# A graph network's first layer: its update from sums split along the node and across it, with products and factors moved into the pair loop

## The chip, the cores and the metric

The kernel runs on one core of a Trainium2 chip. The metric is the device time of one execution in microseconds. Each kernel is run several times and the median is taken.

The engines are PE (TensorE: `matmul` and transposes), DVE (VectorE: elementwise work and reductions), ACT (ScalarE: functions such as sigmoid, logarithm, square root), POOL (GpSimd: elementwise work, and the issue of some transfers) and SP (SyncE, which here only issues transfers). Each has its own queue and works it off in order. SBUF is the memory on the core, 128 partitions wide; PSUM is the memory that PE writes to. A DMA moves data between these and the chip's main memory.

## The reference

Four graph layers run on 4096 nodes with 128 features and one symmetric adjacency matrix of 4096 x 4096. Each is followed by a residual sum and a layer norm. The change concerns the first:

```python
mv = proj(mobius_matvec(weight, x))
h = proj(mobius_add(mv, hyp_bias))                 # 4096 x 128, points of a ball
x_tangent = logmap0(h)
x_local = jax.vmap(lambda xi: logmap(xi, h))(h)    # 4096 x 4096 x 128, never stored
logits = (x_tangent @ wl)[:, None] + (x_tangent @ wr)[None, :] + att_b[0]
adj_att = adj * jax.nn.sigmoid(logits)
support_t = jnp.einsum('ij,ijd->id', adj_att, x_local)
h_agg = proj(expmap(h, support_t))                 # the update
out = proj(expmap0(h_agg))
...
x = _layernorm(x + out)
```

`mobius_add(x, y)` is a sum of x and y with two factors for each row, made from x·x, x·y and y·y. `expmap(h, u)` is `mobius_add(h, tanh(lambda |u| / 2) u / |u|)`. So after the sum over the neighbours all that is left for a node is a combination of two vectors, its own point g and its sum v, with factors that follow from a few scalar products. Layer 1 is an attention of four heads masked by the adjacency; layers 2 and 3 are a normalised product and a second attention.

## The kernel before

**Tiles.** The nodes are 32 row tiles of 128 (`NT`) and 8 blocks of 512 (`NS`). `HA` holds g for all nodes with a column of ones, `HT` its transpose, `X` the sums v and later the layer's output.

**The pair loop** (`Fast.pair_loop`, from L1754). The adjacency is symmetric, so it runs over the 36 block pairs I ≤ J. For each it makes distances on PE (`distance`, L1820 and L1823), the elementwise functions on DVE and ACT (`shift` L1829, `mask` L1849, `square` L1852, `ln` L1856, `root` L1860, `inverse` L1864, `add_root` L1868, `log` L1873, `phi` L1877, `sigmoid` L1837, `first` L1881, `second` L1892), transposes (`turn` L1887), and sums on PE: `sum_i` (L1904) collects in PSUM for row block I over the whole row of pairs, `sum_j` (L1919) gives the part for block J of each pair. `add_j` and `add_i` (L1931 for the first row, L1933 later) bring both into X. After `add_i` of row I, block I is complete, since blocks J > I get their last part from row J.

The order of the engines' queues is written by hand: `SHARED_ORDER` (L43) lists the operations of three pairs, each with its place in the step and how many steps it runs ahead, and `manual_schedule` keeps that order. POOL issues the loads of the rows `el` and `er` (L1806, L1812), which `distance` needs, and DMAs that narrow the adjacency to bf16 in main memory (`adjb`, in `narrow`).

**The update** (the end of `layer0`, L519 to L616). For all 32 tiles, in three passes: the sums `gv` = g·v on DVE (L550) and `vv` = v·v on ACT (L553); then w = wg g + wv v with the sum of its squares (`part` L543 and L545, `w` L569, `junk` L576); then w = c2 w + c1 g, again with the sum of squares (L593, L600); at last X = gf w + x0 (L612) and the layer norm of groups of four tiles (`normalise_tile`, statistics L209 and L210, scaling L244). Between the passes stand chains of small operations on columns of 128 x 32, with square roots and hyperbolic tangents on ACT, for which ACT changes its function table. `x0` is the layer's input, loaded by SP when the loop has ended.

**The proof.** The loop is right only for a symmetric adjacency, and `mirror` (L1691, with `compare` L1698) proves this: it fetches blocks I,J and J,I of `adjb` (512 KB each, `low` and `up`, 48 fetches on SP), PE adds one and subtracts the transpose of the other with identity matrices of different sizes (L1735, L1740), and DVE takes the largest absolute value of the result (L1747). Eight pairs were proved before the loop; the other 20 and the 8 diagonal blocks follow after it. `mirror(ctx)` is called ahead of the three passes, so a planner interleaves both by priority.

**Layer 1** (`Fast.layer1`, L2202). X is transposed on PE (L175, evacuated at L190), queries and keys are multiplied (L2255), each result is cut into two parts (`cut`, ACT L2257, DVE L2258), SP stores 16 pieces of 512 KB to main memory (L2264), and POOL loads them again, stacked for the attention (L2233). Values V (L2271) and residual Y (L2281) follow. Layer 1's preparation takes the priority from which the proof started (`self.rank`). Then comes the attention: scores on PE (`ps` L2045), exponential on ACT (L2052), mask on DVE (`e` L2054), products on PE (`pv` L2071).

Of the kernel before, what the change touches and what calls it, by code (L numbers as in the profile page):

```python
# [9 lines left out]
F32 = mybir.dt.float32  # L10
# [51 lines left out]
class Net:  # L62
# [257 lines left out]
    def layer0(self, x, weight, bias, att_w, att_b):  # L320
# [4 lines left out]
        with ExitStack() as ctx:  # L325
# [191 lines left out]
            pre_pools.close()  # L517
            self.pair_loop(HT, HA, dr, rows, adp, early, rows4)

            x0 = HT.rearrange("p (t d) -> p t d", d=D)
            nc.sync.dma_start(out=x0, in_=self.rows(x))
            late = ctx.enter_context(self.pool(name="late0", bufs=1))
            rot = ctx.enter_context(self.pool(name="rot0", bufs=6))
            self.mirror(ctx)
            w = late.tile([P, NT, D], F32, tag="w", name="w")
            gv, vv, wsq = self.col("gv"), self.col("vv"), self.col("wsq")

            def quadratic(name, a, c):  # L530

                q, r = self.tt(name, a, gg, ALU.mult), self.tt(name + "r", c, gv, ALU.mult)
                nc.vector.scalar_tensor_tensor(q, r, 2.0, q, op0=ALU.mult, op1=ALU.add)
                nc.vector.tensor_tensor(q, q, a, ALU.mult)
                nc.vector.tensor_tensor(r, c, c, ALU.mult)
                nc.vector.tensor_tensor(r, r, vv, ALU.mult)
                nc.vector.tensor_tensor(q, q, r, ALU.add)
                nc.vector.tensor_scalar(q, q, MIN_NORM * MIN_NORM, None, op0=ALU.max)
                return q

            def scaled(t, dst, src, factor):
                if t % 8 in (1, 4, 6):
                    nc.gpsimd.tensor_scalar(dst, src, factor, None, op0=ALU.mult)  # L543
                else:
                    nc.scalar.activation(dst, src, AF.Copy, scale=factor)  # L545

            for t in range(NT):
                k = slice(t, t + 1)
                junk = rot.tile([P, P], F32, tag="junk", name="junk")
                nc.vector.scalar_tensor_tensor(  # L550
                    junk, H[:, t, :], 1.0, X[:, t, :], op0=ALU.mult, op1=ALU.mult, accum_out=gv[:, k]
                )
                junk = rot.tile([P, P], F32, tag="junk", name="junk")  # L553
                nc.scalar.activation(junk, X[:, t, :], AF.Square, accum_out=vv[:, k])
            sm = self.tt("sm", gv, b2x, ALU.mult)
            nc.vector.tensor_tensor(sm, sm, self.XA[:, :, D], ALU.subtract)
            nc.vector.tensor_tensor(sm, sm, bhalf, ALU.mult)


            un = self.norm("un", quadratic("uu", sm, bhalf))  # L560
            th = self.act("sg", self.tt("unb", un, rb, ALU.mult), AF.Tanh)
            sg = self.tt("sgu", th, self.rec("run", un), ALU.mult)
            wg, wv = self.tt("wg", sg, sm, ALU.mult), self.tt("wv", sg, bhalf, ALU.mult)
            nc.vector.tensor_tensor(wg, wg, b, ALU.add)
            for t in range(NT):
                k = slice(t, t + 1)
                part = rot.tile([P, P], F32, tag="part", name="part")
                scaled(t, part, X[:, t, :], wv[:, k])
                nc.vector.scalar_tensor_tensor(w[:, t, :], H[:, t, :], wg[:, k], part, op0=ALU.mult, op1=ALU.add)  # L569
                junk = rot.tile([P, P], F32, tag="junk", name="junk")  # L570
                if t % 4 == 3:
                    nc.vector.scalar_tensor_tensor(
                        junk, w[:, t, :], 1.0, w[:, t, :], op0=ALU.mult, op1=ALU.mult, accum_out=wsq[:, k]
                    )
                else:
                    nc.scalar.activation(junk, w[:, t, :], AF.Square, accum_out=wsq[:, k])  # L576
            den = self.ts("den2", th, -1.0, ALU.mult, 1.0, ALU.add)
            nc.vector.tensor_scalar(th, th, 1.0, None, op0=ALU.add)
            nc.vector.tensor_tensor(den, den, th, ALU.mult)
            nc.vector.tensor_tensor(den, den, b, ALU.mult)  # L580
            nc.vector.tensor_tensor(den, den, wsq, ALU.add)
            nc.vector.tensor_scalar(den, den, MIN_NORM, None, op0=ALU.max)
            rden = self.rec("rden2", den)
            c2 = self.tt("c2", rden, b, ALU.mult)
            c1 = self.tt("c1", rden, wsq, ALU.mult)
            nc.vector.tensor_tensor(c1, c1, b, ALU.mult)

            gsq = self.col("gsq")
            for t in range(NT):
                k = slice(t, t + 1)  # L590
                part = rot.tile([P, P], F32, tag="part", name="part")
                scaled(t, part, H[:, t, :], c1[:, k])
                nc.vector.scalar_tensor_tensor(w[:, t, :], w[:, t, :], c2[:, k], part, op0=ALU.mult, op1=ALU.add)  # L593
                junk = rot.tile([P, P], F32, tag="junk", name="junk")
                if t % 4 == 3:
                    nc.vector.scalar_tensor_tensor(
                        junk, w[:, t, :], 1.0, w[:, t, :], op0=ALU.mult, op1=ALU.mult, accum_out=gsq[:, k]
                    )
                else:
                    nc.scalar.activation(junk, w[:, t, :], AF.Square, accum_out=gsq[:, k])  # L600

            gn = self.norm("gn", gsq)
            gf = self.to_ball("gp", gn)
            gn = self.tt("gn2", gn, gf, ALU.mult)
            nc.vector.tensor_scalar(gn, gn, MIN_NORM, None, op0=ALU.max)
            th = self.act("gth", gn, AF.Tanh)
            nc.vector.tensor_tensor(gf, gf, th, ALU.mult)
            nc.vector.tensor_tensor(gf, gf, self.rec("rgn", gn), ALU.mult)
            nc.vector.tensor_scalar(th, th, MIN_NORM, None, op0=ALU.max)
            nc.vector.tensor_tensor(gf, gf, self.to_ball("gp2", th), ALU.mult)  # L610
            for t in range(NT):
                nc.vector.scalar_tensor_tensor(  # L612
                    X[:, t, :], w[:, t, :], gf[:, t : t + 1], x0[:, t, :], op0=ALU.mult, op1=ALU.add
                )
                if t % 4 == 3:
                    self.normalise_tile(t // 4, on_scalar=True)  # L616
# [1038 lines left out]


class Fast(Net):

    MARKS = 160
    waits = "tile"  # L1660
    banks = 5
    EARLY = 8

    def __init__(self, ctx, tc, x, adj, good):
        super().__init__(ctx, tc, x, adj)
# [81 lines left out]
    def mark(self):  # L1749

        self.marks += 1
        return self.odd[:, self.marks - 1 : self.marks]
# [875 lines left out]
```

## Time and profile before

| what | us |
| --- | --- |
| median of 3 runs | 1984.52 |
| the three runs | 1983.38 to 1991.49 |
| the profiled execution's own time | 1991.43 |
| its span, first to last instruction | 1989.6 |
| last addition into X of the pair loop ends | 639.98 |
| first cut of layer 1 starts | 720.60 |
| last cut of layer 1 (ACT) starts | 751.06 |

The mean granted TensorE clock was 0.968. The last three rows are times from the span's start, in the chain of work that ended last. In what follows, a row of a table by windows gives the stretch in us, its length, and for each engine its busy us and number of instructions; at the end stand the TensorE clock, the share of the DMA engines' time and the GB/s moved. A row of waits names the waiting operation, what it waited for, and the us in total, how many times, and the longest. A row of the chain has the start, the us, and the operation. A row of groups has the line, engine, operation, output and input with their shapes and count, then busy us and mean ns, then the idle time before them with what ended it.

The transfers between the loop's end and 770 are 25 `low` and 17 `up` fetches that fall wholly into it, 16 stores of `qk` with a median of 10.5 us from issue to landing, and 20 loads of the stacks of 256 KB, 11.0 us each.

### The profile page before, as it was taken

What the parts mean: (1) busy time and instruction counts of PE and PEld (TensorE: products, weight loads), DVE (VectorE), ACT (ScalarE), POOL (GpSimd) and SP (SyncE); (2) the same over time, 40 slices, a digit from 0 to 9 for tenths busy, and PEclk for the clock granted to TensorE, in tenths of its full rate; (3) what the DMA queues carried; (4) which work ended last, traced back from release to release, by engine and by line L of the source; (5) the groups of instructions that cost most, each with busy time, mean ns of one, the idle gap of its engine ahead of it and who ended that gap; (6) DMA issues with size and microseconds to landing.
All of it is one profiled execution on the core that took longest, in us unless ns stands there. A gap on an engine that the chain in (4) does not pass through costs nothing.

```text
span 1989.6 us, 23419 instructions
## 1 busy us (share of the span) xinstructions
PE 1843.4 (93%) x8408; PEld 991.9 (50%) x8423; DVE 1737.9 (87%) x2726; ACT 1320.4 (66%) x1671; POOL 174.2 (9%) x275
## 2 busy tenths in 40 slices
PE   6779999999998688999999999999999899899997
PEld 5347676667667354333333333333333566544443
DVE  6689989998898866789999999999998988878896
ACT  5699999999997744778787877778777422210000
POOL 2311111121100411200000000000000000000000
PEclk9889999999999989999999999999999999999999
DMA  9778989898945876986867676867667799968882
GB/s 322 169 144 152 170 134 173 148 177 147 154 119 171 338 248 225 293 252 212 239 212 233 211 233 212 232 214 235 213 215 249 312 421 421 421 245 317 291 283 77
DMA packets 172719, 459.25 MB, mean 231 GB/s; under 512 B 13372, under 2 KB 56156, under 8 KB 148016
## 3 DMA queue, kind: packets, MB, share of 16 engines
q1 hardware_dynamic: 117408, 339.13, 47.3%
q0 software_dynamic: 45824, 50.88, 20.0%
q10 hardware_dynamic: 9360, 67.64, 10.6%
q8 instruction: 68, 1.11, 0.2%
q14 instruction: 59, 0.48, 0.1%
HBM read 480.59 MB, written 111.23 MB: 297 GB/s over the span
## 4 chain that ended last, share of the span: by engine, by line
PE 43%; DVE 28%; ACT 17%; DMA 7%; issue 5%; SPq 0%; POOL 0%; ACTq 0%; DVEq 0%; POOLq 0%
PE pv L2071 11%; PE pa L1586 10%; DVE e L2054 9%; PE ps L2045 6%; ACT e L2052 4%; DMA ring<-adjf 3%; PE pj L1919 3%; PE pi L1904 3%; DVE nat L2036 2%; ACT w L1837 2%; PE pz L1820 2%; DVE t L1868 2%; ACT s L1860 2%; ACT nat L2027 1%; PE pa L2441 1%
## 5 line engine op out<-in xcount | busy, mean ns | idle before, releaser
L2054 DVE SCALAR_TENSOR_TENSOR e<-at,e 128x2048 f32<-128x2048 bf16 x256 | 582.6, 2286 | 76.0 <-ACT e L2052 75.5
L2052 ACT ACTIVATE e<-ps 128x1024 f32<-128x1024 f32 x512 | 493.2, 1024 | 149.4 <-PE ps L2045 122.0
L2071 PE MATMUL pv<-e,VA 128*64 128x512 f32 x2048 | 498.2, 607 | 6.0 <-DVE e L2054 5.5
L2045 PE MATMUL ps<-QS,KS 128*128 128x512 f32 x1024 | 314.2, 424 | 8.7 <-ACT e L2052 8.1
L2045 PEld LDWEIGHTS ps<-QS,KS 128*128 128x128 f32 x1024 | 170.4, 188 | 235.6 <-ACT e L2052 177.6
L2071 PEld LDWEIGHTS pv<-e,VA 128*64 128x64 f32 x2048 | 125.1, 136 | 250.5 <-issue 215.7
L1586 PE MATMUL pa<-w,Y 128*128 128x512 f32 x448 | 195.6, 594 | 0.0
L1583 DVE SCALAR_TENSOR_TENSOR w<-rho,col,ring 128x512 f32<-128x512 f32 x224 | 163.0, 746 | 25.1 <-PE pa L1586 12.3
L1820 PE MATMUL pz<-HT 128*128 128x512 f32 x288 | 160.0, 638 | 18.8 <-DVE w L1892 9.8
L1904 PE MATMUL pi<-HA,w 128*128 128x129 f32 x1152 | 154.9, 283 | 9.4 <-DVE w L1881 9.4
L1904 PEld LDWEIGHTS pi<-HA,w 128*128 128x128 f32 x1152 | 141.7, 196 | 20.8 <-issue 16.8
L2423 PE MATMUL pa<-ring,Y 128*128 128x512 f32 x512 | 132.3, 409 | 14.5 <-DVE ring L2398 10.0
L1586 PEld LDWEIGHTS pa<-w,Y 128*128 128x128 f32 x448 | 83.6, 190 | 106.4 <-issue 79.2
L2027 ACT ACTIVATE nat<-nat 128x2048 f32<-128x2048 f32 x64 | 122.6, 1915 | 4.9 <-DMA nat<-in_adj_dram 4.9
L1919 PE MATMUL pj<-HA,w 128*128 128x129 f32 x896 | 118.1, 288 | 2.2 <-DVE X L1933 1.1
L2423 PEld LDWEIGHTS pa<-ring,Y 128*128 128x128 f32 x512 | 95.9, 192 | 44.3 <-DVE ring L2398 12.8
L1919 PEld LDWEIGHTS pj<-HA,w 128*128 128x128 f32 x896 | 110.5, 201 | 10.4 <-issue 7.4
L1829 DVE TENSOR_SCALAR t<-pz 128x512 f32<-128x512 f32 x144 | 93.4, 683 | 14.9 <-PE pz L1823 14.9
L1868 DVE SCALAR_TENSOR_TENSOR t<-t,s 128x2048 f32<-128x2048 f32 x36 | 82.3, 2285 | 20.8 <-ACT s L1860 20.8
L1837 ACT ACTIVATE w<-di,dr 128x512 f32<-128x512 f32 x144 | 90.6, 707 | 0.3 <-DMA di<-rows 0.2
L1892 DVE TENSOR_TENSOR w<-w,ptz 128x512 f32<-128x512 f32 x112 | 73.6, 682 | 18.2 <-PE ptz L1887 17.8
L2387 DVE SCALAR_TENSOR_TENSOR odd<-ring 128x1024 bf16<-128x1024 f32 x64 | 78.1, 1220 | 10.0 <-DMA ring<-adjf 9.5
(419 smaller groups left out, 2351.9 us busy)
## 6 DMA issues: line engine op xcount, KB each, us to landing
ring<-adjf SPq DMA_DIRECT2D x128, 1024.0 KB, 13.8
adjf<-in_adj_dram SPq DMA_DIRECT2D x64, 1024.0 KB, 6.8
nat<-in_adj_dram ACTq DMA_DIRECT2D x64, 1024.0 KB, 5.5
ad<-in_adj_dram SPq DMA_DIRECT2D x36, 1024.0 KB, 8.5
adjb<-in_adj_dram POOLq DMA_DIRECT2D x64, 512.0 KB, 11.6
at<-adjb SPq DMA_DIRECT2D x63, 512.0 KB, 3.5
low<-adjb SPq DMA_DIRECT2D x28, 512.0 KB, 5.2
up<-adjb SPq DMA_DIRECT2D x20, 512.0 KB, 6.3
```

What stands on the lines that cost most here:

```text
L1583: nc.vector.scalar_tensor_tensor(w, rho[:, I * S : (I + 1) * S], col[:, 0, j : j + 1], at[:, jb, :], op0=ALU.max, op1=ALU.mult)
L1586: nc.tensor.matmul(pa, lhsT=F[:, j, :], rhs=w, start=False, stop=(j == NT - 1), skip_group_check=True)
L1820: nc.tensor.matmul(pz, lhsT=HT[:, j * P : (j + 1) * P], rhs=HT[:, I * S : (I + 1) * S], start=True, stop=False)
L1837: nc.scalar.activation(w[:, jb, :], st[p]["d"][k], AF.Sigmoid, bias=dr[:, 4 * J + jb : 4 * J + jb + 1])
L1904: nc.tensor.matmul(row[I, "po"][ib // 2][:, ib % 2, :], lhsT=st[p]["w0"][:, jb, ib * P : (ib + 1) * P], rhs=HA[:, 4 * J + jb, :], start=False,
L1919: nc.tensor.matmul(pj[:, a, :], lhsT=st[p]["w1"][:, ib, jb * P : (jb + 1) * P], rhs=HA[:, 4 * I + ib, :], start=(ib == 0), stop=(ib == 3),)
L2027: nc.scalar.activation(nat, nat, AF.Identity, accum_out=self.deg2[:, k, i : i + 1])
L2045: nc.tensor.matmul(p[:, h, :], lhsT=KS[:, h2 + h, jb * P : (jb + 1) * P], rhs=QS[I % 2][:, h2 + h, :], start=True, stop=True,)
L2052: nc.scalar.activation(e[:, h2 : h2 + 2, :], p, AF.Exp)
L2054: nc.vector.scalar_tensor_tensor(e, at[:, jb % 4, :].unsqueeze(1).to_broadcast([P, NH, S]), 0.0, e, op0=ALU.not_equal, op1=ALU.mult,)
L2071: nc.tensor.matmul(st["po"][h // 2][g : g + 64, :], lhsT=VA[:, o : o + 64], rhs=e[:, h, :], start=(jb == 0), stop=(jb == NT - 1), skip_gro ...
L2423: nc.tensor.matmul(st["pa"], lhsT=halves[k][:, j, :], rhs=at[:, jb, :], start=(I > 0 and j == k == 0), stop=(j == NT - 1 and k == 1), skip ...
```

## The change

The sum v is split into a part along g and a part across it. With gv = g·v and gg = g·g, `along` = -gv/gg, and v + along g is the part across, with ss its square. The update's result is then x0 + ga g + gb (v + along g), with factors ga and gb that follow from gv, ss and gg alone, by column work. No vector w is formed, and no pass takes sums of it.

Blocks of rows 0 to 6 (28 row tiles) are split within the pair loop. As soon as `add_i` has completed block I, the generator `apart(I)` issues a product on POOL; six places of the written order later a reduction and a small product on DVE, and three products on POOL; ten places later a second reduction on DVE. `proceed` is called at each place and also advances `factors` for the first 16 tiles (`SPLIT = 4` blocks) by one small operation, where the square root is made as an exponential of half a logarithm, so that it uses the table that ACT has loaded; hyperbolic tangents are made behind the sigmoids. The first four tiles' outputs are finished in the loop's last part, on DVE.

After the loop follow the sums of the last four tiles, `factors` for the other 16 tiles with square roots, with row tiles between its steps, then the remaining tiles: two fused operations, statistics and scaling. All of this is under `manual_schedule`. Only then is `self.mirror(ctx)` called, where it stood ahead of the passes. `x0` is loaded where the loop's order issues its last loads. The old passes remain as `Net.update`, for the program that runs only where the proof fails.

In the queues that result, SP has 36 of the 48 proof fetches, then the 16 stores, then the other 12 fetches, where all 48 stood ahead of the stores. PE has 306 of the 521 matmuls of the proof ahead of the first query and key product, 36 among these products, 18 among those of the values, 21 about the bound of the scores, and 140 behind the attention's first six scores, where all stood ahead.

```diff
             pre_pools.close()
+            self.given = x, HT, HA, gg, b, rb, b2x, bhalf
             self.pair_loop(HT, HA, dr, rows, adp, early, rows4)
-            x0 = HT.rearrange("p (t d) -> p t d", d=D)
-            nc.sync.dma_start(out=x0, in_=self.rows(x))
-            self.mirror(ctx)
...
+            self.update(ctx)
...
@@ class Fast @@
+    SPLIT = 4
...
+    def factors(self, lo, hi, logs):
...
+        def root(t):
+            nc.vector.tensor_scalar(t, t, MIN_NORM * MIN_NORM, None, op0=ALU.max)
+            yield "root"
+            if logs:
+                nc.scalar.activation(t, t, AF.Ln)
+                nc.scalar.activation(t, t, AF.Exp, scale=0.5)
+            else:
+                nc.scalar.activation(t, t, AF.Sqrt)
...
+        tt(ga, c2, a)
+        tt(gb, c2, q)
...
+    def update(self, ctx):
...
+        def tiles(lo, hi):
+            for t in range(lo, hi):
+                x = X[:, t, :]
+                nc.vector.scalar_tensor_tensor(x, x, gb[:, t : t + 1], x0[:, t, :], op0=ALU.mult, op1=ALU.add)
+                nc.vector.scalar_tensor_tensor(x, HA[:, t, 0:D], ga[:, t : t + 1], x, op0=ALU.mult, op1=ALU.add)
+                self.row_stats(t)
...
+        with self.tc.manual_schedule():
+            tiles(0, 4)
+            last = range(NT - 4, NT)
...
+            for hop in self.factors(4 * self.SPLIT, NT, False):
+                if hop in ("sums", "tanh") and hops < 2 or hop == "root" and hops:
+                    tiles(made, made + 1 + (hops > 0))
+                    made += 1 + (hops > 0)
...
+            for I in range(self.NS):
+                tiles(max(made, 4 * I), 4 * I + 4)
+                if I:
+                    scale(I - 1)
+            scale(self.NS - 1)
+        self.mirror(ctx)
...
@@ Fast.pair_loop @@
+            dotp = ctx.enter_context(self.pool(name="dot0", bufs=1))
+            self.cols_of_update()
+            ahead_of = self.factors(0, 4 * self.SPLIT, True)
+            due, hop = [], None
...
                     for k, po in enumerate(row[I, "po"]):
                         add_up(I, I, k, po)
+                    self.complete = I + 1
+                    if I < NS - 1:
+                        due.append([0, apart(I)])
...
+            def apart(I):
+                c = slice(4 * I, 4 * I + 4)
+                g, v = HA[:, c, 0:D], self.X[:, c, :]
+                prod = dotp.tile([P, 4, D], F32, tag="prod", name="prod")
+                nc.gpsimd.tensor_tensor(prod, g, v, ALU.mult)
+                yield 6
+                nc.vector.tensor_reduce(self.gv[:, c], prod, AX.X, ALU.add)
+                nc.vector.tensor_tensor(self.along[:, c], self.gv[:, c], self.minus[:, c], ALU.mult)
+                prod = dotp.tile([P, 4, D], F32, tag="prod", name="prod")
+                nc.gpsimd.tensor_tensor(prod, g, self.along[:, c].unsqueeze(2).to_broadcast([P, 4, D]), ALU.mult)
+                nc.gpsimd.tensor_tensor(v, v, prod, ALU.add)
+                prod = dotp.tile([P, 4, D], F32, tag="prod", name="prod")
+                nc.gpsimd.tensor_tensor(prod, v, v, ALU.mult)
+                yield 10
+                nc.vector.tensor_reduce(self.ss[:, c], prod, AX.X, ALU.add)
...
+            def proceed(last):
+                nonlocal hop
+                for d in due:
+                    d[0] -= 1
+                if due and due[0][0] <= 0:
+                    wait = next(due[0][1], None)
+                    if wait is not None:
+                        due[0][0] = wait
+                    else:
+                        due.pop(0)
+                        if self.complete >= self.SPLIT:
+                            hop = hop or ""
...
+                hop = next(ahead_of, "end") or ""
...
                 for i in range(-max(reach), n // UNIT - min(reach)):
                     step(i)
+                    if i + max(reach) == n // UNIT - 1:
+                        nc.sync.dma_start(out=x0, in_=self.rows(self.given[0]))
+                while due or hop != "end":
+                    proceed(True)
```

## The prediction

> **What bounds the kernel now.** I read the page's table of engines first (PE 93% busy, DVE 87%, ACT 66% of 1989.6 us), and set it aside: it averages four layers, and the change touches only layer 0 and the step into layer 1. The stages matter, so the second view is the table by windows: the pair loop (79 to 640 us), the three passes of the update, and layer 1's preparation until its attention starts at 767.
>
> ```profile
> core 0: us, PE busy (x) PEld busy (x) DVE busy (x) ACT busy (x) POOL busy (x), PEclk, DMA share, GB/s
> 160.00:600.00 440.00, 424.33 (x2445) 298.30 (x2444) 406.88 (x390) 426.57 (x380) 72.04 (x118) 0.97 0.86 151
> 640.00:648.00 8.00, 6.44 (x72) 4.44 (x69) 8.00 (x64) 7.36 (x51) 0.00 (x0) 1.00 0.79 268
> 648.00:668.30 20.30, 13.97 (x138) 8.76 (x140) 17.11 (x80) 17.37 (x79) 8.35 (x12) 1.00 1.01 381
> 668.30:688.70 20.40, 13.47 (x137) 8.76 (x140) 16.97 (x62) 17.56 (x73) 11.85 (x13) 1.00 1.01 394
> 688.70:720.60 31.90, 21.89 (x190) 16.37 (x194) 24.93 (x130) 15.64 (x44) 0.00 (x0) 0.84 0.45 149
> 720.60:753.00 32.40, 25.07 (x92) 15.00 (x91) 21.82 (x34) 11.47 (x17) 10.90 (x20) 0.84 1.03 332
> 753.00:767.00 14.00, 10.88 (x82) 9.40 (x81) 9.39 (x20) 3.42 (x4) 0.00 (x0) 1.00 0.98 350
> ```
>
> In the loop three engines are nearly full together: ACT 426.57 of 440 (97%), PE 96%, DVE 406.88 (92%). DVE has 33 us to spare, ACT 13. The two middle passes of the update run at a DMA share of 1.01: the symmetry proof's 48 fetches stream beside them. Third view: the waits of ACT and the chain after the loop.
>
> ```profile
> ACT y L1852 <- DVE t L1829: 4.1, 3, 2.9
> ACT t L1873 <- DVE t L1868: 1.1, 4, 0.3
> ```
> ```profile
> 703.85 5.01 DMA low<-adjb
> ...
> 712.08 4.17 DMA low<-adjb
> ...
> 720.60 0.70 ACT cut L2257
> ...
> 728.35 9.41 DMA qk<-cut
> ...
> 739.37 11.58 DMA qk<-cut
> ```
>
> ACT waits for DVE only 5.2 us in 440: DVE is just fast enough. After the loop the chain goes through the columns and passes, then through the proof's fetches (PE's queue holds all of some 520 proof matmuls ahead of the first query/key product), then through the stores of the query/key pieces, which saturate the DMA (332 to 350 GB/s). So the update lies wholly on the path, and what comes behind it is bound by DMA.
>
> **What the Trainium skill says.** "SBUF — State Buffer", section "Who interferes with whom": GpSimd shares its port pair with DVE, a DVE instruction with two SBUF inputs contends with a GpSimd one that reads SBUF, the pair is an exclusive lock, and tensor_reduce never contends. The trace agrees in the one place where both run, before the loop:
>
> ```profile
> 49.87 1.05 DVE L499 TENSOR_TENSOR de<-de,ah 128x32 f32<-128x32 f32 x1
> ```
> ```profile
> 49.84 1.04 POOL L462 TENSOR_TENSOR squares<-HA 128x512 f32<-128x512 f32 x1 [14.33 <-DVE HA L457]
> ```
>
> A 128x32 product (0.18 to 0.19 us elsewhere) took as long as the GpSimd product beside it. "GPSIMD Engine Reference", section 4.1, says that two-input elementwise work is about twice as slow there; no run here shows one operation on both engines. "ScalarE: Activation LUTs", "What ACT_TABLE_LOAD costs", has 1283 ns a load; the trace has 1.28 us, and both kernels issue 215 loads.
>
> **The change part by part.**
>
> *1. Work put into the loop.* For each of rows 0 to 6 the new generator `apart` puts four GpSimd products of 128x512 (1.04 us each by the row above), two DVE reductions (128x512 to 4: 0.68 us, the size of L1829's 683 ns) and one tiny DVE product (0.18) into queues written by hand. Between them stand these DVE rows:
>
> ```profile
> L1829 DVE TENSOR_SCALAR t<-pz 128x512 f32<-128x512 f32 x118 | 76.2, 683 | 5.9 <-PE pz L1823 5.9
> L1868 DVE SCALAR_TENSOR_TENSOR t<-t,s 128x2048 f32<-128x2048 f32 x29 | 66.3, 2285 | 9.5 <-ACT s L1860 9.5
> L1877 DVE TENSOR_TENSOR t<-t,y 128x2048 f32<-128x2048 f32 x29 | 66.2, 2283 | 0.0
> ```
>
> The operations of 2.28 us read two SBUF operands and so lock GpSimd out; shifts (L1829) and the additions from PSUM (0.42) do not. Rows 1, 2, 4, 5: add_root starts just as the first product is issued, which waits 2.28 and then takes 1.04; the reduction, next in DVE's queue, waits about 1.0. Then 0.68 + 0.18. The second product fits under an addition and a shift (1.1); phi then locks out the third. The second reduction, right behind phi, waits for the third and fourth products, 2.1 to 2.3, then 0.68. Sum 1.0 + 0.86 + 2.2 + 0.68, with a little for semaphores: 5.1 us. Rows 0, 3, 6 have only PSUM work in between: about 1.5 of operations and 1.8 of waits, 3.3. In all 4 x 5.1 + 3 x 3.3 = 30 us of DVE time. `factors` for the first 16 columns adds 48 small DVE operations of 0.11 to 0.18 (their spacing in the columns at 648 to 653, independent or dependent): 6.5 us. Together 37 us, against DVE's 33 to spare in 160:600 and 58 idle in the whole loop.
>
> What shows? ACT's next square comes only 0.3 to 2.6 us after the shift that feeds it (at row 1's end the last shift ends at 361.45, the square starts at 362.31). A delay of 3.3 to 5.1 less such a lead leaves about 2.5 each, 7 x 2.5 = 17.5, and ACT at 97% cannot make it up. The small operations come singly and mostly fit: 1.5. I take 19. Bounds: 5 if the buffers between DVE and ACT soak it up (37 fits in 58), 37 if none does. Queued behind the GpSimd products are the edge loads (el, er) and the narrow copies of the adjacency: el for pair 12 was issued at 214.05 and would now be issued near 242, with 4.2 us to land and PE needing it at 246.4. Just in time; 0 to 3 us, inside the 19's upper bound.
>
> *2. The update gets shorter.* Removed: the pass of sums over 28 tiles, the w pass, the second pass (8 + 20.3 + 20.4 us with their columns). Left after the loop: four tiles' sums and squares (about 3 us), the factor columns of 16 tiles (about 45 operations, 0.22 where one needs the last, three reciprocals of 0.35, five table switches of 1.28: about 17 us, of which eight row tiles fill the waits), and 20 or so further tiles on DVE at two fused products of 0.27, bn 0.22 and aggregation 0.13: 0.9 to 1.1 each with their waits (rows of the last pass), 20 us; then scaling, transposes and the first product. About 54 us from the loop's end to the first cut, where the profile has 720.60 - 639.98 = 80.6. The proof does not hold it up: only about 306 of the 520 proof matmuls now stand before the first product on PE, 36 fetches on SP before the stores, and these 18.9 MB are 48 us at the 394 GB/s of the second pass. Gain 26; bounds 22 to 30.
>
> *3. The proof is emitted after the update.* Twelve of the 48 fetches (512 KB each, 6.3 MB) now stand behind the 16 stores on SP, and about 140 proof matmuls on PE behind the first scores of the attention and ahead of the rest. At the 383 GB/s of this stage 6.3 MB are 16.4 us. They start when the last store is issued, 32 us after the first cut (752.9), and share the DMA with the loads of the stack. Before, attention's first product on DVE came 46.2 us after the first cut (766.8); I expect 57 to 60. Cost 12. Bounds: 4 if the stores' waits leave gaps for them, 20 if they wait for buffers and run after the loads. The DMA agrees: between the loop's end and 770 lie the proof's 25 MB, 16 stores (8.4 MB) and 20 stack loads of 256 KB (5.2 MB), 101 us at 383 GB/s, against 127 now. So 2 and 3 together cannot bring more than 26, and stores cannot begin before the update ends; I have 14.
>
> Same in both: the x load's place in SP's queue (2 MB), layers 1 to 3, the loops' other DMAs. Edits with no time of their own: the method split, the constants of the columns (3 small operations before the loop).
>
> Sum: +19 - 26 + 12 = +5. The profiled execution took 1991.43 (span 1989.6), at the top of its three runs; against the median 1984.52 this gives about 1990, +0.3%. A measurement of this kernel can tell some 0.5%, 10 us, from no change.
>
> **The rivals.**
> - *The loop swallows the work.* For it: 58 us of DVE idle time in the loop, three t and two y buffers. Against it: ACT at 97% and the short lead. Loop +5, update -26, proof +6: -15, 1969.5.
> - *Slower, by the port lock in the loop.* One mechanism: where a GpSimd product meets a 2.28 us DVE operation, each holds the other up, and the in-order DVE queue passes the whole delay to ACT. For it: the 1.05 us row, and 37 us of added DVE time against 33. Against it: idle time elsewhere in each step. Loop +35, with -26 and +12: +21, 2005.5. It decides once the loop grows by more than 24, which is where the sum passes 10.
> - *The proof's tail blocks the attention fully.* PE's 140 proof matmuls wait for fetches that share the DMA with at loads: +20 instead of 12: +13, 1997.5.
>
> **How the numbers follow.** Forecast (within 10 us of before, a few slower) 0.37; loop swallows 0.27; port lock 0.27; proof's tail 0.09. Some of the forecast's own spread lies over the bound, some of the last two below it: faster 0.27, same 0.35, slower 0.38. The likeliest case alone has 1978 to 2000; the range reaches to both neighbours, 1965 to 2011.
>
> **What would show it.** The loop's end (last X addition from pi at 639.22) near 658; DVE waits for GpSimd at the two reductions, near 1 and 2 us, seven times; ACT waiting for shifts in tens of us instead of 4.1. First cut 54 us after the loop's end. Low and up fetches behind the qk stores, and the first attention product on DVE 57 to 60 after the first cut. I am wrong if the loop ends before 650, or if attention starts less than 50 us after the first cut, or if the update takes over 65.

## The result, and the profile after

The changed kernel takes 2042.91 us (median of 4 runs, 2039.32 to 2044.3), beside 1988.01 for the kernel before (median of 4 runs, 1983.38 to 1991.49). The ratio is 1.0275, with a 95% interval of 1.0244 to 1.0306. The profiled execution has a span of 2041.7 us, 52.1 more than before.

The first view is the table by windows of the changed kernel: the loop (which now ends at 699.7), the stretch up to the first cut at 756.8, and from there until the attention runs at 827.

```profile
160.00:600.00 440.00, 403.36 (x2226) 282.85 (x2225) 378.40 (x398) 386.82 (x348) 93.43 (x126) 0.93 0.75 140
600.00:699.70 99.70, 82.02 (x462) 65.45 (x460) 83.93 (x96) 69.36 (x61) 28.08 (x26) 0.85 0.44 119
699.70:709.70 10.00, 5.03 (x34) 3.54 (x36) 9.52 (x45) 5.67 (x13) 1.91 (x1) 0.66 0.10 27
709.70:756.80 47.10, 32.39 (x304) 22.12 (x308) 36.97 (x150) 20.06 (x49) 0.00 (x0) 1.00 0.91 329
756.80:827.00 70.20, 53.94 (x377) 39.08 (x381) 34.22 (x57) 16.29 (x21) 10.90 (x20) 0.91 0.94 330
```

In 160:600 ACT's busy time fell from 426.57 to 386.82 and DVE's from 406.88 to 378.40, although DVE has more to do. PE falls from 424.33 to 403.36 too. The three engines that the prediction found nearly full stand more: this is a loss by waiting, not by work. (GpSimd alone is busier, 93.43 beside 72.04, and the granted clock is 0.93 beside 0.97; whether the clock is more than a consequence of the waits is not shown. The median matmul of `pz` takes 497 ns in both.) The loop's last addition from pi starts at 699.3, where it started at 639.6, first before, then changed:

```profile
L1933 DVE TENSOR_TENSOR X<-X,pi x14: 415/417/423, 340.5 to 639.6; 128x258 f32<-128x258 f32 x14
L2108 DVE TENSOR_TENSOR X<-X,pi x14: 390/415/417, 351.6 to 699.3; 128x258 f32<-128x258 f32 x14
```

That is +59.7. From there to the first cut 57.5 pass, 81.0 before: -23.5. From the first cut to the attention's first pv product 72.9 pass (756.8 to 829.7), 49.7 before (720.6 to 770.3): +23.2. The sum is +59.4; the rest of the program is 7 shorter (attention 787.2 instead of 790.8, and 3.7 after it), which no experiment pursued.

Who waits in the loop? The next fences are views of single tiles, el and dj, each in the kernel before and then in the changed kernel: idle us before their readers, and how often, by what ended it; then the us from a transfer's issue to its landing.

```profile
  DMA el<-rows: 3.0, 3
DMA to landing us min/median/max: 1.7/4.2/16.1
  DMA dj<-rows: 5.4, 4
DMA to landing us min/median/max: 5.7/8.4/11.0
```
```profile
  DMA el<-rows: 27.1, 8
DMA to landing us min/median/max: 1.7/8.0/19.6
  DMA dj<-rows: 36.7, 9
DMA to landing us min/median/max: 5.6/9.0/15.4
```

The row of el counts PE's weight loads and its matmuls apart, often for one and the same wait, so it serves to compare kernels and not as PE's lost time. (The landing of 16.1 before lies ahead of 100 us; from 100 to 700 the longest is 8.5 before and 19.6 in the changed kernel.) These are the waits of the matmuls alone, before and changed:

```profile
PE pz L1820 <- DMA el<-rows: 1.5, 1, 1.5
PE pz L1998 <- DMA el<-rows: 11.6, 3, 4.0
```

Waits for loads have come up, in a loop whose own transfers have not changed. The timeline of GpSimd shows why. First the kernel before around the end of row 1, then the changed kernel at the same point (start, us, line, operation, and the idle time before it with what ended it).

```profile
323.42 1.03 POOL L1812 DMA_DIRECT2D el<-rows  x2 [13.05 <-PE pz L1823]
330.63 1.00 POOL L1812 DMA_DIRECT2D el<-rows  x2 [6.18 <-PE pz L1823]
331.62 1.50 POOL L1962 DMA_DIRECT2D adjb<-in_adj_dram  x2
333.11 1.04 POOL L1806 DMA_DIRECT2D er<-rows  x2
348.59 0.98 POOL L1812 DMA_DIRECT2D el<-rows  x2 [14.44 <-PE pz L1823]
```
```profile
352.46 3.19 POOL L2153 TENSOR_TENSOR prod<-HA,X 128x512 f32<-128x512 f32 x1 [32.72 <-DVE X L2108]
356.71 1.04 POOL L2158 TENSOR_TENSOR prod<-HA,v 128x512 f32<-128x512 f32 x1 [1.06 <-DVE v L2156]
357.83 3.11 POOL L2159 TENSOR_TENSOR X<-X,prod 128x512 f32<-128x512 f32 x1
361.02 1.04 POOL L2161 TENSOR_TENSOR prod<-X 128x512 f32<-128x512 f32 x1
362.00 1.50 POOL L2140 DMA_DIRECT2D adjb<-in_adj_dram  x2
363.50 2.02 POOL L1987 DMA_DIRECT2D el<-rows  x4
365.51 1.50 POOL L2140 DMA_DIRECT2D adjb<-in_adj_dram  x2
369.80 0.52 POOL L1981 DMA_DIRECT2D er<-rows  x1 [2.79 <-DMA adjb<-in_adj_dram]
```

GpSimd's queue issues loads ahead of their use; in the kernel before it only stands until PE has freed a buffer of el. Now the first product waits for `add_i` on DVE, and GpSimd stands 32.72 us at it. Of what is queued behind, two el pairs and four narrow copies of 512 KB are issued in one bunch from 362 on. Then GpSimd stands again, until a narrow copy has landed, ahead of each of the two er loads (2.79 and 3.94). PE waits for el until 374.74, and ACT for a dj that SP issued at 365.5, just beside the bunch (9.84 us idle at 378.49). GpSimd's waits over the whole loop (79 to 705 us), the kernel before first:

```profile
POOL el L1812 <- PE pz L1823: 384.6, 30, 22.0
```
```profile
POOL prod L2153 <- DVE X L2108: 187.9, 6, 41.8
POOL el L1987 <- PE pz L1998: 177.3, 15, 20.0
POOL prod L2153 <- DVE X L2106: 39.2, 1, 39.2
POOL adjb L2140 <- DMA adjb<-in_adj_dram: 28.5, 9, 3.6
POOL er L1981 <- DMA adjb<-in_adj_dram: 21.1, 5, 5.1
```

The idle time at el shows the queue's lead: it stands there when it has issued all that the buffers allow. Of 384.6 us 177.3 are left, and 227.1 are spent at the seven first products. With two smaller rows (4.7 and 4.4), GpSimd further waits 58.7 us for copies or loads of its own, adjb, el or er, to land. All seven kernels here that put products waiting for `add_i` at that place of GpSimd's queue have such waits in this window, 55 to 59 us; the other eleven have none. Why the queue stands there is not shown.

### The profile page after: what moved, and what is told of

The parts are those of the page before. It is cut to its first block, busy times and chain, and to the rows that moved or that the text cites. A ratio compares the mean times of both kernels' runs of the same rounds, so it can differ in the third digit from the quotient of the medians.

```text
span 2041.7 us, 23159 instructions
## 1 busy us (share of the span) xinstructions
PE 1860.9 (91%) x8407; PEld 1010.7 (50%) x8423; DVE 1740.4 (85%) x2659; ACT 1288.4 (63%) x1485; POOL 202.6 (10%) x280
## 4 chain that ended last, share of the span: by engine, by line
PE 39%; DVE 27%; ACT 16%; DMA 11%; issue 4%; POOL 2%; SPq 0%; ACTq 0%; DVEq 0%; POOLq 0%
PE pv L2296 11%; PE pa L1589 9%; DVE e L2279 9%; PE ps L2270 6%; DMA ring<-adjf 4%; ACT e L2277 4%; DMA dj<-rows 3%; ACT w L2012 3%; DVE nat L2261 2%; PE pj L2094 2%; ACT s L2035 2%; ACT y L2031 2%; PE pz L1995 2%; ACT nat L2252 1%; PE pi L2079 1%
## 5 line engine op out<-in xcount | busy, mean ns | idle before, releaser
L1995 PE MATMUL pz<-HT 128*128 128x512 f32 x288 | 166.4, 661 | 20.0 <-DVE t L2004 15.5
L2079 PE MATMUL pi<-HA,w 128*128 128x129 f32 x1152 | 164.3, 295 | 8.9 <-DVE w L2056 8.9
L2079 PEld LDWEIGHTS pi<-HA,w 128*128 128x128 f32 x1152 | 151.3, 208 | 20.5 <-issue 19.2
L2094 PE MATMUL pj<-HA,w 128*128 128x129 f32 x896 | 122.2, 295 | 2.4 <-DVE w L2067 1.8
L2004 DVE TENSOR_SCALAR t<-pz 128x512 f32<-128x512 f32 x144 | 93.7, 682 | 19.6 <-PE pz L1998 19.6
L2012 ACT ACTIVATE w<-dj,dr 128x512 f32<-128x512 f32 x112 | 71.6, 709 | 36.8 <-DMA dj<-rows 36.7
```

The lines of the kernel that those rows point to most:

```text
L1995: nc.tensor.matmul(pz, lhsT=HT[:, j * P : (j + 1) * P], rhs=HT[:, I * S : (I + 1) * S], start=True, stop=False)
L2012: nc.scalar.activation(w[:, jb, :], st[p]["d"][k], AF.Sigmoid, bias=dr[:, 4 * J + jb : 4 * J + jb + 1])
L2079: nc.tensor.matmul(row[I, "po"][ib // 2][:, ib % 2, :], lhsT=st[p]["w0"][:, jb, ib * P : (ib + 1) * P], rhs=HA[:, 4 * J + jb, :], start=False,
L2094: nc.tensor.matmul(pj[:, a, :], lhsT=st[p]["w1"][:, ib, jb * P : (jb + 1) * P], rhs=HA[:, 4 * I + ib, :], start=(ib == 0), stop=(ib == 3),)
```

## The experiments

Each row gives the start of the loop's last addition from pi, and the time from there to the start of the first pv product of the attention, from the profiled execution; then the ratio to the kernel before with its interval.

| kernel | last addition | to first pv | ratio |
| --- | --- | --- | --- |
| before | 639.6 | 130.7 | |
| changed | 699.3 | 130.4 | 1.0275 [1.0244, 1.0306] |
| no_loop | 641.8 | 130.3 | 1.0019 [1.0003, 1.0035] |
| proof_ahead | 702.1 | 130.2 | 1.0286 [1.0264, 1.0308] |
| tiny_products | 671.9 | 132.1 | 1.0145 [1.0122, 1.0168] |
| products_on_dve | 683.1 | 132.0 | 1.0201 [1.0179, 1.0224] |
| rows_ahead | 690.2 | 131.6 | 1.0247 [1.0226, 1.0268] |
| before_rows_ahead | 629.2 | 131.5 | 0.9964 [0.9951, 0.9976] |
| factors_only | 643.1 | 128.2 | 0.9996 [0.9981, 1.0011] |
| products_only | 693.1 | 130.4 | 1.0265 [1.0242, 1.0287] |
| before_no_proof | 637.8 | 129.5 | 0.9988 [0.9973, 1.0002] |
| after_no_proof | 698.5 | 104.7 | 1.0173 [1.012, 1.0225] |
| late_products | 658.2 | 148.4 | 1.0161 [1.0111, 1.0212] |
| lock_alone | 639.5 | 129.2 | 1.0017 [1.0001, 1.0033] |
| queue_alone | 682.9 | 130.2 | 1.0232 [1.0205, 1.026] |
| dve_alone | 646.6 | 130.3 | 1.006 [1.0036, 1.0083] |
| late_products_only | 655.7 | 146.2 | 1.0128 [1.009, 1.0165] |
| after_loop_best | 632.0 | 130.2 | 0.9958 [0.9945, 0.9971] |

### Is it the loop, or what follows?

**no_loop.** `apart` is not called, and the sums of all tiles are taken after the loop:

```diff
-                        due.append([0, apart(I)])
...
+            for I in range(self.NS):
...
+                for t in range(4 * I, 4 * I + 4):
...
+            for _ in self.factors(0, NT, False):
+                pass
```

> All sums and all factors after the loop, in the new form (no w passes); nothing added in the pair loop. If the loss lies in the loop, the loop ends again at about 640 (699.7 in the changed kernel) and the update, with 32 tiles' sums (32 x 0.27 twice) more on DVE, takes about 68 instead of 57; the time falls to 1970 to 1985. Rival, the loss lies in the update and the proof's tail: the loop's end at 640 but the time still above 2000.

The last addition is back at 641.8. What follows is no shorter than before: 130.3. The expected time of 1970 to 1985 is missed just above (1991.25 beside 1986.85), because the update did not take the expected 68: the first cut starts 80.1 after the last addition, beside 81.0 before. The loss is the loop's, and the new update by itself, all after the loop, has won nothing. Whether its own work or the proof beside it holds it there was not tried.

**proof_ahead.** The rank from which layer 1's preparation takes its priority is read after the proof instead of ahead of it:

```diff
-        self.proof, self.rank = ExitStack(), self.tc.cur_priority
+        self.proof = ExitStack()
...
         self.compare(self.proof, pairs, False)
+        self.rank = self.tc.cur_priority
```

> The changed kernel with layer 1's preparation ranked behind the proof, so that all 48 fetches stand ahead of the last stores and no proof matmul stands in the attention's queue. If the 140 proof matmuls in the attention cost what the trace says (ACT idle 12.4 and 6.8 around them, first pv 73 us after the first cut against 50), the time falls by 8 to 15 against the changed kernel, to about 2030. Rival, the transfers bind whatever their order: within 4 us of 2043.

The rival was right: 2046.26, within 4 of the changed kernel, and 130.2 from the last addition to pv. The proof matmuls are gone from the attention, but the first cut came at 760.8 and the last stores after 811. Between these two orders the time only moves from one place to the other.

**before_no_proof and after_no_proof.** `mirror` opens no pool and fetches nothing:

```diff
-        self.compare(self.proof, pairs, False)
```

> The kernel before without the proof after the loop (its 48 fetches, matmuls and reductions are left out). From the loop's end to the attention's first pv product it takes 130 us in the kernel before. If the update is what lies on that path, the proof only beside it, the stretch stays within 8 of 130. If the transfers of the proof bind it, it falls to 95 to 112.

> The changed kernel without the proof after the loop. If the proof hides the shorter update, this stretch (130 us in both kernels) falls further than in the kernel before without the proof, by the 20 to 25 us that the update lost: 75 to 92. If the update's shortening is worth nothing, both fall alike (within 6 of each other).

In the kernel before, the proof is wholly hidden: 129.5 without it. There the update holds the path. In the changed kernel it is not hidden: 104.7 without it, 130.4 with it. (The expected 75 to 92 was missed, for the kernel before did not get shorter without the proof; the further fall, expected at 20 to 25, came.) So the shorter update is worth 24.8 (129.5 - 104.7) where no proof stands beside it, and 0.3 (130.7 - 130.4) where one does. The fence shows the changed kernel's scalar engine at the place where the tail of the proof is met.

```profile
802.89 1.28 ACT L2277 ACT_TABLE_LOAD   x1 [14.77 <-PE ps L2270]
804.18 1.94 ACT L2277 ACTIVATE e<-ps 128x1024 f32<-128x1024 f32 x2
806.14 1.28 ACT L2410 ACT_TABLE_LOAD   x1
819.84 1.02 ACT L2277 ACTIVATE e<-ps 128x1024 f32<-128x1024 f32 x1 [12.42 <-PE pm L1744]
827.64 2.86 ACT L2277 ACTIVATE e<-ps 128x1024 f32<-128x1024 f32 x3 [6.77 <-PE ps L2270]
```

The first exponential starts at 804.18, and the attention then stands, but for one more at 819.84, until 827: 12.42 us end with a proof matmul (pm) and 6.77 with the scores queued behind those. Meanwhile the chain has its transfers:

```profile
789.92 10.23 DMA up<-adjb
...
801.72 6.10 DMA low<-adjb
809.48 4.33 DMA low<-adjb
...
815.49 8.15 DMA low<-adjb
```

### Which part of the work in the loop?

**factors_only and products_only.** One leaves the generator's work out and keeps the small operations, the other is the reverse.

```diff
-                prod = dotp.tile([P, 4, D], F32, tag="prod", name="prod")
-                nc.gpsimd.tensor_tensor(prod, g, v, ALU.mult)
                 yield 6
...
                 yield 10
-                nc.vector.tensor_reduce(self.ss[:, c], prod, AX.X, ALU.add)
```
```diff
-    SPLIT = 4
+    SPLIT = 0
...
-                        if self.complete >= self.SPLIT:
-                            hop = hop or ""
```

> The changed kernel without the generator's products and reductions in the loop (the sums of 28 tiles are left out, their columns hold zeros), so that only the 48 small DVE operations and the ACT steps of the first 16 columns stay in the loop. If the products are the loss, the loop ends at 645 to 652; if the round trips between DVE and ACT in the factors are, at 665 or later.

> The changed kernel with all factors after the loop (32 columns at once, no early tiles), the products of seven row blocks in the loop as they are. If the products are the loss, the loop ends at 680 to 695; if the factors' round trips are a large part, at 675 or earlier.

643.1, which is 3.5 more than before (a little below the expected 645), and 693.1, which is 53.5 more and within its range. The generator's work, the products with the reductions that read them, is the loss.

**lock_alone, queue_alone and dve_alone** put single parts of it into the kernel before, each at the generator's places.

```diff
                         add_up(I, I, k, po)
+                    if I < NS - 1:
+                        g = HA[:, 4 * I : 4 * I + 4, 0:D]
+                        for _ in range(4):
+                            prod = dotp.tile([P, 4, D], F32, tag="prod", name="prod")
+                            nc.gpsimd.tensor_tensor(prod, g, g, ALU.mult)
```

This is lock_alone. In queue_alone the loop runs over `k` and has another last line:

```diff
+                            nc.gpsimd.tensor_tensor(prod, g, g if k else self.X[:, 4 * I : 4 * I + 4, :], ALU.mult)
```

dve_alone has no products. Six places of the order after `add_i`, and again ten places after that, it has these lines:

```diff
+                        nc.vector.tensor_reduce(s4, HA[:, 4 * I : 4 * I + 4, 0:D], AX.X, ALU.add)
+                        if not stage:
...
+                            nc.vector.tensor_tensor(s5, s4, s4, ALU.mult)
```

> The kernel before with 28 added GpSimd products of the same size in the same places, which read HA alone: they wait for nothing, nothing reads them, and DVE has no more to do. It shows the port lock by itself. If the lock costs DVE what the products take, 28 x 1.04 and more, the loop ends at 655 or later; if not, within 8 of 639.98.

> The kernel before with the 28 GpSimd products of lock_alone, where the first product of each row now reads X and so waits for add_i on DVE; nobody reads the results and DVE has no more to do. The one difference to lock_alone (loop's end 639.9) is that the products stand at the head of GpSimd's queue until DVE has come that far. If the blocked queue by itself is a main loss, the loop ends at 655 to 675 and PE's waits for el rise from 3.8 to over 15; if it hurts only together with DVE's waits, it ends within 8 of 640.

> The kernel before with only the two reductions and the small product of each row on DVE at the generator's places, reading data that is long there, so without a wait and without GpSimd: 7 x 1.5 = 10.7 us more for DVE. If DVE's time reaches ACT in full, the loop ends at about 651; if DVE's idle time takes it, within 4 of 640.

Both engines slow each other down, and it costs the loop nothing here. These are groups of lock_alone between 160 and 620: GpSimd's products took 2137 ns each instead of 1.04 us alone, and the masks on DVE 2409 ns instead of 2287.

```profile
L1948 POOL TENSOR_TENSOR prod<-HA 128x512 f32<-128x512 f32 x28 | 59.8, 2137 | 1.8
L1850 DVE TENSOR_TENSOR t<-t,ad 128x2048 f32<-128x2048 f32 x31 | 74.7, 2409 | 0.4
```

But the last addition starts at 639.5, as before. Between 160 and 620 DVE is busy 432.41 us beside 425.79 before; its idle time took the difference. In queue_alone a single operand of seven instructions differs from lock_alone, and nobody reads the result; the last addition starts at 682.9, 43.4 later and beyond the expected 675. The waits of PE for el, and of DVE:

```profile
PE pz L1824 <- DMA el<-rows: 29.9, 5, 10.3
```
```profile
DVE t L1830 <- PE pz L1824: 36.7, 23, 6.5
DVE w L1893 <- PE ptz L1888: 30.4, 17, 5.2
```

PE's matmuls wait 29.9 us for el (3.0 in lock_alone), the shifts on DVE wait 36.7 for PE (14.2), and ACT's squares 32.0 for the shifts (5.1). The blocked queue does this alone. The slower operations of DVE are not in it: its masks take 2395 ns and phi 2338, about 5 us more in all than before, and lock_alone bore more than that. dve_alone ends at 646.6, +7.0 for 10.7 us of added work, between its two expectations.

**tiny_products and products_on_dve.**

```diff
-                nc.gpsimd.tensor_tensor(prod, g, v, ALU.mult)
+                nc.gpsimd.tensor_tensor(prod, g[:, :, 0:4], v[:, :, 0:4], ALU.mult)
```
```diff
-                nc.gpsimd.tensor_tensor(prod, g, v, ALU.mult)
+                nc.vector.tensor_tensor(prod, g, v, ALU.mult)
```

The other three products of a row are changed likewise, the first diff in tiny_products, the second in products_on_dve.

> The changed kernel with every GpSimd product cut to 4 of 128 columns: the same waits and places in the queues, hardly any port time. Leaves out most of the sums and of the part across, so the output is another. Theory 1, GpSimd's queue blocked by products that wait for DVE, with el, er and the narrow copies late behind them: the loop still ends at 685 to 700. Theory 2, port lock and product time: it ends at 645 to 665.

> The changed kernel with the four products of each row on DVE, at the same places: GpSimd's queue is as in the kernel before. 28 products of some 0.65 us are 18 us more on DVE. Theory 1 (blocked queue): the loop ends at 655 to 670, earlier than 699.7 although DVE has more to do. Theory 2 (DVE's own time and its waits): 685 or later.

Neither met its numbers. Tiny products still cost 32.3, more than theory 2 and less than theory 1 allowed: the view of el has 11.8 instead of 27.1, which fits a queue that is let go sooner (the four full products held it from 352.46 to 362.00). But the two reductions on DVE got shorter too, and their waits for GpSimd fell from 16.1 to 0.4, so this run does not tell the queue from DVE's share. With the products on DVE the queue is free (el 3.0), but the loop ends 43.5 later than before: DVE has about 19 us of products more (28 of 0.69), beside reductions and factors, and ACT waits 31.1 for dj. At these places of the order both engines are bad places for this work.

**rows_ahead, before_rows_ahead, late_products and late_products_only.** The loads of the distance rows move up in the written order: `rows.0.0.3` from behind `load.0.0.3` to ahead of `load.0.2.2`, the other two (as `rows.0.1.3` and `rows.0.2.3`) to ahead of `load.0.1.3`. late_products also puts 110 places (the order has 117) before the first and the second product, and starts the factors only when four blocks are wholly split:

```diff
-edges.0.1.3 inverse.0.2.2 shift.2.0.3 turn.1.1.2 sum_i.2.0.2 shift.3.0.3 load.0.0.3 shift.0.0.3 rows.0.0.3
+edges.0.1.3 inverse.0.2.2 shift.2.0.3 turn.1.1.2 sum_i.2.0.2 shift.3.0.3 load.0.0.3 shift.0.0.3
...
-                        due.append([0, apart(I)])
+                        due.append([110, apart(I)])
...
                 nc.vector.tensor_tensor(self.along[:, c], self.gv[:, c], self.minus[:, c], ALU.mult)
+                yield 110
...
-                        if self.complete >= self.SPLIT:
+                        self.parted = getattr(self, "parted", 0) + 1
+                        if self.parted >= self.SPLIT:
```

> The changed kernel, with the loads of the distance rows (di, dj) issued up to a third of a step earlier in SP's queue, ahead of the adjacency load that waits for mask on DVE. Nothing else moves. Theory: a delay of DVE reaches ACT mainly through SP (mask late, ad issued late, dj behind it late; ACT waits 36.7 for dj). Then ACT's waits for dj and di fall from 44 to under 10 and the loop ends 20 to 35 earlier, at 665 to 680. Rival: dj is late only because the whole step is; then the waits turn into waits for DVE (shift, mask) and the loop ends within 8 of 699.7.

> The kernel before with the same move of the row loads, as a control. ACT waits only 5.4 for dj there, so the loop ends 0 to 8 earlier than 639.98, and the time falls by no more than 8.

> The changed kernel with the row loads ahead, and the GpSimd products put about one step (110 places) later in the written order, before the first and again before the second product, so that GpSimd does not stand waiting for DVE with el, er and the narrow copies behind it. The same products, reductions and factors. With the row loads ahead alone the loop ended at 690.6 and PE waited 52.0 for el. If the blocked queue is the main loss, PE's waits for el fall below 10 and the loop ends at 640 to 660. Rival, DVE's work and the port lock: 675 or later.

> late_products with all factors after the loop. late_products' loop ended at 658.6, 29 later than the kernel before with the row loads ahead (629.6), and ACT waited 27 for factor columns. If the factors' round trips are that rest, the loop ends at 634 to 645; if DVE's reductions and the products are, at 650 or later.

In rows_ahead dj is no longer waited for, but the loop ends only 9.1 earlier, where the theory had 20 to 35 and the rival at most 8: the rival's mechanism came, the wait has changed its name. The first fence is of ACT's waits, the second of el, both in rows_ahead:

```profile
ACT y L2027 <- DVE t L2004: 44.0, 5, 16.9
```
```profile
  DMA el<-rows: 52.0, 8
```

The same move takes 10.4 off the kernel before, more than the 8 expected, so it is a gain of its own and not a cause of the loss. With the products late, the wait for el falls to 4.5, GpSimd's idle time at el is back at 361.7, and the last addition moves from 690.2 to 658.2: 32 less, with the same products on the same engine, and within the expected 640 to 660. (Rows 5 and 6 are then finished behind the loop, hence the 148.4.) Against before_rows_ahead 29 remain. They are hardly the factors (late_products_only, 655.7). They grow evenly: row 1's addition at 340.5 beside 335.2 of before_rows_ahead, row 4's at 578.3 beside 560.0, the last at 655.7 beside 629.2. Reductions, locked products and waits for them were not taken apart further there; the cause of these 26.5 stays open.

**after_loop_best** joins the edits of no_loop, of the row loads ahead, and of proof_ahead, with `mirror` called ahead of the update's tiles:

```diff
         nc.gpsimd.memset(eps, EPS_LN)
+        self.mirror(ctx)
...
             scale(self.NS - 1)
-        self.mirror(ctx)
```

> A candidate: nothing added in the loop, the row loads ahead, the new update after the loop (sums of all 32 tiles, one pass of tiles), the proof ahead of layer 1's preparation. The loop ends at about 630. If the gaps in the proof's stream (transposes that wait on PE ahead of proof matmuls) are what keep loop's end to first pv at 130, this falls to 118 to 126 and the time to 1966 to 1976; if not, 1978 to 1984, as the kernel before with the row loads ahead.

1979.98, 0.4% below the kernel before (0.9958), but before_rows_ahead has nearly the same (0.9964, with an interval that overlaps): the gain looks like that of the row loads. The stretch after the loop stayed at 130.2, so the expected filling of the proof's gaps did not come.

## Why the prediction was wrong

**The step that failed is the loop's cost, within part 1.** It had 19, with bounds of 5 and 37; it is 59.7. Its DVE arithmetic was fair: the reductions wait 16.1 us for GpSimd in all, where its waits add up to 18 (4 of 1.0, 4 of 2.2, 3 of 1.8). The second reduction stands 2.19 us behind GpSimd, as worked out. These are rows of DVE around the end of row 4:

```profile
614.50 0.67 DVE L2155 TENSOR_REDUCE v<-prod 128x4 f32<-128x512 f32 x1
...
616.22 2.48 DVE L2052 TENSOR_TENSOR t<-t,y 128x2048 f32<-128x2048 f32 x1
...
620.89 0.69 DVE L2163 TENSOR_REDUCE v<-prod 128x4 f32<-128x512 f32 x1 [2.19 <-POOL prod L2161]
```

What failed is the sentence on what is queued behind the products, "Just in time; 0 to 3 us". It saw that el would be issued some 28 us late (its 242 came true, at 242.27), and priced it with the median landing of an undisturbed kernel, 4.2. It did not count that narrow copies and a second el pair go out in the same bunch, that landings of el would go to a median of 8.0 and a maximum of 19.6, and that the queue would stand another 58.7 us behind its own transfers. How much of the loss each of the two brings was not taken apart. queue_alone measures the term as a whole, in the kernel before: 43.4 instead of 0 to 3. With dve_alone's 7.0 and the factors' 3.5 that makes 54 of 59.7, if such parts may be added; the waits of the two reductions were not measured alone. One sign also failed: ACT was to wait tens of us for the shifts. In the changed kernel it waits 6.2 for them and 36.7 for dj; only when the row loads move ahead do the waits for shifts come (44.0).

**The port lock was the wrong rival.** The page "SBUF — State Buffer" of the Trainium skill, section "Who interferes with whom", describes it, and lock_alone shows it on both engines; but it decided nothing. In the changed kernel DVE's masks take 2285 ns, as before (2287). The rival was right in its sign alone: it had +35 for the loop by another mechanism, and its 2005.5 is 37 too low.

**Part 2 was right**: 57 us to the first cut where 54 was forecast, and a gain of 23.5 where it said 26. The same prices did not carry to no_loop, where 68 was expected and 80.1 came, so a good part of the hit may be luck.

**Part 3 had the mechanism and half its size.** 12 was forecast, with an upper bound of 20; it is 23.2 at the first pv product, and the first product on DVE, forecast 57 to 60 after the first cut, comes 70.5 after it (827.3). The attention starts its scores and stops in the middle, as the order of PE's queue said. The sum of the two, a gain of 14, is 0.3. The check by bytes (not more than 26 to win) let 14 pass; it took the stream to be full at 383 GB/s from the loop's end, where it moved 27 GB/s in the first 10 us and about 329 after. From the loop's end to the attention the mean is 306 GB/s, and it was 302 before, where the prediction's own table has 149 at 688.70 and 332 to 350 behind. At such a mean the same 39 MB take about as long as before, and nothing is left to win.

**The time and the chances.** 1990 with a range to 2011 missed 2042.91. The three parts were added as if the first could only be a matter of DVE and ACT, the two engines that the view of waits named. Two smaller points of the prediction do not stand either. The profiled execution of each kernel has 43 table loads; 215 stands in neither. And products_on_dve shows what no run had shown, one operation on both engines: a product takes 0.69 us on DVE and 1.04 to 1.27 at best on GpSimd, 1.5 to 1.8 times as long and not quite twice.

## What to carry to other kernels

An instruction that waits, put into the queue of an engine that issues loads ahead of time, took that lead away from all of them here: price it as the lead lost (227.1 us at seven rows), plus the bunch that follows, and not by its own duration. Before moving work to an idle engine, look at what that engine's queue does when it is idle. And where a pass hides a stream of transfers, a shorter pass may only uncover the stream, as here: take the stream out in an experiment first, to see what the pass is worth.

## What was not expected of the hardware

GpSimd's product of 128x512 took 1.04 us at best and 2.1 on average beside a full DVE, up to 3.3 in the changed kernel. In lock_alone 59.8 us of such products cost the loop nothing. And el, a load of 2 x 512 numbers, landed between 100 and 700 us in 4.2 at the median and 8.5 at most before, but in 8.8 and up to 19.6 in the changed kernel, where it is issued next to a few copies of 512 KB from the same queue.
